# A graph network's edge loop on TensorE: the second layer's banks between the first layer's groups

## The chip, the core and the metric

One core of a Trainium2 chip runs the whole kernel in one launch. Its engines run side by side and wait for each other through semaphores: TensorE (PE in the profile; its weight loads have a row of their own, PEld) multiplies, VectorE (DVE) and ScalarE (ACT) work element by element, GpSimd (POOL) here issues the gathers, SyncE (SP) issues most other transfers. TensorE writes to PSUM, eight banks of 2 KB a partition; VectorE and ScalarE carry its results on to SBUF.

The metric is the device time of one execution in microseconds, as the median of several runs.

## The reference

A layer of message passing over a graph of 6250 nodes and 100000 edges, sorted by destination, with a residual and a normalisation behind it:

```python
row, col = edge_index[0], edge_index[1]                     # source, destination
msg_in = concatenate([x[row], x[col]], axis=-1)             # 100000 x 256
h = relu(msg_in @ Wm1 + bm1)                                # 256 wide
h = relu(h @ Wm2 + bm2)                                     # 256 wide
messages = h @ Wm3 + bm3                                    # 128 wide
agg = segment_sum(messages, col) / clip(count(col), 1)
upd = relu(concatenate([x, agg]) @ Wn1 + bn1) @ Wn2 + bn2
out = layernorm(x + (x + upd))
```

Everything is float32.

## The kernel before

The first layer's product is split: `x @ Wm1` is computed once for each node, for the source half (table `atab`, float32) and for the destination half (table `btab`, three bfloat16 terms that add up to a float32). This prologue takes about the first 90 us. Per edge the first layer is then a sum of two table rows. The third layer is linear, so it is applied after the sum over edges, once for each node.

The edges go in 196 groups of 512 (four tiles of 128), two groups a step, 98 steps; step p's stages are spread over several turns of the loop at L978, so that in one turn TensorE works on four steps. In turn p, TensorE does this, in the order in which it is written down (its order is the program's: `manual_schedule` holds PE from L285, ACT and POOL from L287 and DVE from L525 to it):

- **turning** (`turned`, L760, matmul L770) of step p-3: six transposes of the summed rows, 64 rows by 64 columns of the array each, into two banks; VectorE adds them to the accumulator `acc` (`pair_window`, L739, or `add_up`, L774);
- **node steps** of spot 0 (`node_steps`, L930): pieces of the work on finished nodes, dealt out from turn 34 on;
- **first layer** (`first_layer`, L660) of step p: for both groups the *rows*, 16 transposes a group of the gathered rows of `atab` into `ph` (L666), and then for both groups the *products* of `btab` rows with a one-hot matrix of the destinations, added in `ph` (L674, four a group in the early steps; L683, eight a group from step 59 on). `ph` takes four of the eight PSUM banks, two for each group, and there is one `ph`. ScalarE then applies bias and relu in two instructions, each over both groups (L692), into one of two tiles `h1`;
- **sums** (`summed`, L948; `pair_sums`, L729, matmul L734, in the last steps `sums`, L718, matmul L724) of step p-2: 16 matmuls, 32 columns of the array each, which add the edges of a window of nodes from `h2s`, four side by side. ScalarE copies the result (`part_of`, L748, copy L752);
- **second layer** (`second_layer`, L706, matmul L711) of step p-1: for each group two banks of eight matmuls on the whole array. VectorE takes each bank's maximum with the negated bias into `h2s` (L714), one tile for each group. Between the first group's two banks and the second's stand the node steps of spot 1.

The other four PSUM banks are handed out in turn by `bank()` (L562): whoever asks gets the bank that was handed out four calls before, and waits until that one's reader is done. A turn asks seven times (two for the turning, one for the sums, four for the second layer), more with node steps.

`fetch` (L598) issues the loads of step p+1 in turn p: eight gathers on POOL's queue (L607), four for each group, and four, later eight, loads of `btab` rows on SP's queue (L620). The first SP load waits for the last product that read the same buffer (two steps before). Three of the gathers also wait for a mark of TensorE (`MARKS`, L587), which keeps them in its pace: the first for the sums' last matmul, the fifth for a matmul at the start of the fourth bank, the seventh for the first product.

`follows` and `keep` (L572, L580) leave out waits that other waits already imply.

Of the kernel before, what the change touches and what calls it, by code (L numbers as in the profile page):

```python
# [20 lines left out]
P = 128  # L21
# [9 lines left out]
def kernel(  # L31
# [511 lines left out]
    with edge, tc.tile_pool(name="wk", bufs=2) as wk, tc.tile_pool(  # L543
# [116 lines left out]
        def first_layer(got, ohts, nts, step):  # L660
            for i, ((ag, _, _), nt) in enumerate(zip(got, nts)):
                for c in range(HC):
                    for j in range(GT):
                        for h in range(nt // 2):
                            half = slice(h * HP, (h + 1) * HP)
                            nc.tensor.matmul(ph[:, i, h, c, j * HP:(j + 1) * HP], ag[half, j, c * P:(c + 1) * P],  # L666
                                             ident[half, half], is_transpose=True, start=(c == 0 and j == 0),
                                             stop=False, skip_group_check=True)
            for i, ((_, bw, paired), nt) in enumerate(zip(got, nts)):
                for c in range(HC):  # L670
                    if paired:
                        for h in range(2):
                            half = slice(h * HP, (h + 1) * HP)
                            matmul = nc.tensor.matmul(ph[:, i, h, c, :], bw[half, 0, c * P:(c + 1) * P],  # L674
                                                      ohts[half, i, :], start=False, stop=True,
                                                      skip_group_check=True)
                            pace(step + 1, "products", (i * HC + c) * 2 + h, matmul)
                            last_product[step] = matmul
                        continue
                    for k in range(2):  # L680
                        for h in range(nt // 2):
                            half = slice(h * HP, (h + 1) * HP)
                            matmul = nc.tensor.matmul(ph[:, i, h, c, k * P:(k + 1) * P],  # L683
                                                      bw[half, k, c * P:(c + 1) * P],
                                                      ohts[half, i, k * P:(k + 1) * P], start=False, stop=True,
# [292 lines left out]
        for i in range(NP + 7):  # L978
# [42 lines left out]
            if p == 0:  # L1021
                whole(x_part(X_FIRST, bank, (nc.scalar, nc.vector)))
# [100 lines left out]
```

## Time and profile before

| | us |
|---|---|
| median of 3 runs | 1339.16 |
| lowest and highest | 1331.02, 1341.98 |
| the profiled execution, its own time | 1348.45 |
| its span, first to last instruction | 1346.7 |
| TensorE busy, of the span | 1237.1 |
| GpSimd busy | 793.6 |
| VectorE busy | 618.8 |
| ScalarE busy | 335.5 |
| mean granted TensorE clock | 0.976 |

Times inside the profile count from the span's start. In a row of the timeline stand the start, the length of what is merged in it, the engine, the line of the kernel, the operation, what it writes and reads, the shape, the number of instructions, and in brackets the engine's idle time before it with what ended it. A matmul's start is recorded and its end is modelled, and matmuls overlap, so the pitch from start to start tells more than the mean length. In the groups, "idle before" is the idle time of the engine just before such instructions. "Issue" means that the engine waited for nothing that the profile shows.

### The profile page before, as it was taken

The page shows a single profiled execution, that of the slowest core. Times are in us where ns is not written, and L with a number is a line of the kernel's source. Part 1 is how long each engine was busy: PE and PEld are TensorE (multiplying, and loading weights), DVE is VectorE, ACT ScalarE, POOL GpSimd, SP SyncE. Part 2 cuts the span into 40 slices and gives each one's busy share as a digit, 9 for nine tenths or more (in the row PEclk, how much of TensorE's full clock was granted, in tenths as well). Part 3 has the DMA queues.
Part 4 walks back from the last instruction along what each step waited for, and adds up shares of the span by engine and source line. Part 5 has one row for each costly group of instructions (what it writes and reads, how often), then busy time and mean ns, then how long its engine had stood idle before and what let it go on. Part 6 is the DMA issues. An engine that isn't in the chain of part 4 may idle for free.

```text
span 1346.7 us, 26320 instructions
## 1 busy us (share of the span) xinstructions
PE 1237.1 (92%) x10288; PEld 935.8 (69%) x10289; DVE 618.8 (46%) x1502; ACT 335.5 (25%) x500; POOL 793.6 (59%) x854
## 2 busy tenths in 40 slices
PE   8988998999999999999999998989988999999996
PEld 6746666776776667766766766767767677777784
DVE  6754333333333334443444443534445454555675
ACT  4741221122122112222221222221222212223232
POOL 6666665665666666666666665655655655556531
PEclk9999999999999999999999999999999899999998
DMA  7963443433433334334343444434444434344320
GB/s 224 336 207 105 124 116 99 114 106 101 112 108 112 101 107 115 106 108 129 108 110 113 123 114 118 134 111 125 131 115 120 123 111 137 107 118 122 108 58 24
DMA packets 113876, 163.66 MB, mean 122 GB/s; under 512 B 24730, under 2 KB 74592, under 8 KB 113728
## 3 DMA queue, kind: packets, MB, share of 16 engines
q0 software_dynamic: 38160, 103.75, 27.5%
q1 hardware_dynamic: 67292, 44.97, 10.8%
q10 hardware_dynamic: 8292, 13.18, 3.4%
q8 instruction: 82, 1.34, 0.4%
q14 instruction: 50, 0.41, 0.1%
HBM read 142.35 MB, written 19.86 MB: 120 GB/s over the span
## 4 chain that ended last, share of the span: by engine, by line
PE 89%; issue 6%; DVE 4%; DMA 0%; ACT 0%; POOL 0%; DVEq 0%; SPq 0%; ACTq 0%; POOLq 0%
PE bank L711 53%; PE bank L734 11%; PE ph L666 9%; PE bank L770 3%; PE ph L674 2%; PE pbt L315 2%; PE ph L683 2%; PE bank L844 2%; PE bank L811 1%; PE bank L817 1%; PE bank L724 1%; PE pxu L426 1%; DVE h L714 1%; DVE acc L779 0%; DVE span_i L267 0%
## 5 line engine op out<-in xcount | busy, mean ns | idle before, releaser
L607 POOL DMA_INDIRECT rows<-atab,srcT x784 | 746.1, 952 | 485.2 <-issue 166.8
L711 PE MATMUL bank<-w,h 128*128 128x256 f32 x3128 | 722.6, 386 | 8.0 <-DVE h L714 4.1
L711 PEld LDWEIGHTS bank<-w,h 128*128 128x128 f32 x3128 | 592.5, 192 | 139.3 <-issue 52.5
L714 DVE TENSOR_TENSOR h<-bank,nb 128x512 f32<-128x512 f32 x391 | 264.9, 690 | 600.8 <-PE bank L711 407.4
L692 ACT ACTIVATE h<-ph,b 128x1024 f32<-128x1024 f32 x194 | 205.6, 1110 | 789.2 <-remote 393.5
L666 PE MATMUL ph<-ident,rows 64*128 64x64 f32 x3128 | 134.6, 226 | 38.1 <-issue 36.6
L734 PE MATMUL bank<-h,oh 128*32 128x257 f32 x1312 | 155.5, 409 | 12.4 <-issue 1.3
L666 PEld LDWEIGHTS ph<-ident,rows 64*128 64x128 f32 x3128 | 117.2, 141 | 49.7 <-issue 46.5
L734 PEld LDWEIGHTS bank<-h,oh 128*32 128x32 f32 x1312 | 46.8, 112 | 93.8 <-issue 77.1
L743 DVE TENSOR_TENSOR acc<-acc,bank 128x96 f32 x328 | 83.5, 255 | 40.2 <-remote 18.4
L770 PEld LDWEIGHTS bank<-ident,part 64*128 64x128 f32 x681 | 31.1, 137 | 48.1 <-issue 27.6
L770 PE MATMUL bank<-ident,part 64*128 64x64 f32 x681 | 46.8, 237 | 12.6 <-DVE h L714 8.6
L315 PE MATMUL pbt<-w,xT 128*128 128x256 f32 x196 | 47.6, 388 | 5.9 <-DVE rest L340 3.0
L752 ACT COPY part<-bank 128x257 f32<-128x257 f32 x114 | 42.1, 375 | 24.4 <-PE bank L711 17.3
L315 PEld LDWEIGHTS pbt<-w,xT 128*128 128x128 f32 x196 | 36.5, 194 | 13.4 <-DVE rest L340 4.2
L674 PE MATMUL ph<-oht,rows 64*128 64x256 bf16 x472 | 40.1, 275 | 4.2 <-issue 4.2
L683 PE MATMUL ph<-oht,rows 64*128 64x128 bf16 x620 | 32.7, 225 | 10.7 <-issue 10.0
L642 DVE TENSOR_TENSOR oh<-iota_w,dloc 128x256 f32<-128x256 f32 x82 | 34.3, 418 | 0.0
L779 DVE TENSOR_TENSOR acc<-acc,bank 128x63 f32 x126 | 27.8, 221 | 13.3 <-remote 4.5
L683 PEld LDWEIGHTS <-rows 64*128 64x128 bf16 x620 | 23.2, 99 | 14.8 <-issue 14.7
L640 DVE TENSOR_SCALAR oht<-db,iota_p 128x512 bf16<-128x512 bf16 x98 | 31.8, 324 | 0.0
L674 PEld LDWEIGHTS <-rows 64*128 64x128 bf16 x472 | 24.4, 97 | 7.2 <-issue 6.3
(167 smaller groups left out, 613.0 us busy)
## 6 DMA issues: line engine op xcount, KB each, us to landing
rows<-btab SPq DMA_DIRECT2D x544, 32.0 KB
db<-reltab ACTq DMA_DIRECT2D x98, 128.0 KB
rows<-atab,srcT POOLq DMA_INDIRECT x784
btab<-acc SPq DMA_DIRECT2D x24, 384.0 KB
atab<-at SPq DMA_DIRECT2D x24, 256.0 KB
x_sb<-in_x_dram SPq DMA_DIRECT2D x5, 512.0 KB
xd<-in_x_dram SPq DMA_DIRECT2D x6, 256.0 KB
out_dram<-xd SPq DMA_DIRECT2D x6, 256.0 KB
```

Source lines behind the costliest of these rows:

```text
L315: nc.tensor.matmul(pbt[:, a, :], xT[:, (t0 + a) * P:(t0 + a + 1) * P], w1[:, k, :], start=True, stop=True)
L607: gather = nc.gpsimd.indirect_dma_start(out=ag[:, j, :], out_offset=None, in_=atab[:, :], in_offset=bass.IndirectOffsetOnAxis(ap=idx[:, j: ...
L666: nc.tensor.matmul(ph[:, i, h, c, j * HP:(j + 1) * HP], ag[half, j, c * P:(c + 1) * P], ident[half, half], is_transpose=True, start=(c == ...
L674: matmul = nc.tensor.matmul(ph[:, i, h, c, :], bw[half, 0, c * P:(c + 1) * P], ohts[half, i, :], start=False, stop=True, skip_group_check= ...
L683: matmul = nc.tensor.matmul(ph[:, i, h, c, k * P:(k + 1) * P], bw[half, k, c * P:(c + 1) * P], ohts[half, i, k * P:(k + 1) * P], start=Fal ...
L692: made = [nc.scalar.activation(h1[:, :, c, :].rearrange("p i (h e) -> p i h e", h=2), ph[:, :, :, c, :], AF.Relu, bias=b1[:, c:c + 1]) for ...
L711: matmul = nc.tensor.matmul(ph2[:, j - j0, :], h1[:, c, j * P:(j + 1) * P], w2[:, c, :], start=(c == 0), stop=(c == HC - 1))
L714: made = nc.vector.tensor_tensor(h2[:, j0:j0 + 2, :H], ph2, nb2.to_broadcast([P, 2, H]), op=ALU.max)
L734: matmul = nc.tensor.matmul(pg[(2 * i + q) * WN:(2 * i + q + 1) * WN, :H + 1], oh[:, 2 * q + k, :], h2[:, 2 * q + k, :], start=k == 0, sto ...
L743: made = nc.vector.tensor_add(window, window, pts[q // 2][:, 0, :, k:k + WN])
L752: copied.append(nc.scalar.copy(part[:nt * WN, i], pg[:nt * WN, :H + 1]))
L770: nc.tensor.matmul(pts[r][:, i, c, :], rows, ident[half, half], is_transpose=True, start=True, stop=True, skip_group_check=True)
```

## The change

The loop's turn is written in another order, and four functions are cut up for it; no instruction is added or taken away. `first_layer` becomes `first_group`, called once for each group (rows, then products of that group), and `relus`. `second_layer` becomes `second_bank` (eight matmuls) and `largest` (the VectorE part); the first group's two banks are now issued one by one. The order of TensorE in a turn is then:

turning, node steps of spot 0, first group's rows and products, **bank 1**, sums, **bank 2**, second group's rows and products, node steps of spot 1, **banks 3 and 4**.

With it move: `fetch` from behind the whole first layer to behind its first group; the relus to behind the second group, and so behind the sums' copy in ScalarE's order; the VectorE part of bank 1 to behind the sums; in turn 0 a piece of prologue work (`x_part`), and in the last turn the loading of window starts (`load_firsts`), from before the second group's banks to before the node steps of spot 1. The loop over further windows behind the main loop, which is skipped when no window needs it, calls the same functions.

```diff
         def first_layer(got, ohts, nts, step):
-            for i, ((ag, _, _), nt) in enumerate(zip(got, nts)):
...
+            for i in range(len(nts)):
+                first_group(i, got, ohts, nts, step)
+            return relus(nts, step)
+
+        def first_group(i, got, ohts, nts, step):
+            (ag, bw, paired), nt = got[i], nts[i]
+            for c in range(HC):
+                for j in range(GT):
+                    for h in range(nt // 2):
+                        half = slice(h * HP, (h + 1) * HP)
+                        nc.tensor.matmul(ph[:, i, h, c, j * HP:(j + 1) * HP], ag[half, j, c * P:(c + 1) * P],
+                                         ident[half, half], is_transpose=True, start=(c == 0 and j == 0),
+                                         stop=False, skip_group_check=True)
+            for c in range(HC):
+                if paired:
...
+        def relus(nts, step):
             h1 = next_h1()
...
         def second_layer(h1, h2, nt, step, before):
             for j0 in range(0, nt, 2):
...
+                largest(second_bank(h1, j0, step, before), h2, j0)
+
+        def second_bank(h1, j0, step, before):
+            ph2 = bank()
+            for j in range(j0, j0 + 2):
+                for c in range(HC):
+                    matmul = nc.tensor.matmul(ph2[:, j - j0, :], h1[:, c, j * P:(j + 1) * P],
+                                              w2[:, c, :], start=(c == 0), stop=(c == HC - 1))
+                    pace(step + 2, "second", before + j * HC + c, matmul)
+            return ph2
+
+        def largest(ph2, h2, j0):
+            made = nc.vector.tensor_tensor(h2[:, j0:j0 + 2, :H], ph2, nb2.to_broadcast([P, 2, H]), op=ALU.max)
+            follows("copied", made)
+            keep("largest", made)
...
-            if p < NP:
-                s = st[p]
-                s["h1"] = first_layer(s.pop("got"), s.pop("ohts"), s["nts"], p)
+            now = st[p] if p < NP else None
+            was = st[p - 1] if 0 <= p - 1 < NP else None
+            if now:
+                first_group(0, now["got"], now["ohts"], now["nts"], p)
             if i < NP:
                 st[i]["got"] = fetch(i, [(srcT[:, 2 * i + k, :], firsts[k]) for k in range(2)], [q for q, _ in queues],
                                      paces.pop(i, {}))
-            if p == 0:
-                whole(x_part(X_FIRST, bank, (nc.scalar, nc.vector)))
+            ph2 = second_bank(was["h1"][:, 0], 0, p, 0) if was else None
             if 0 <= p - 2 < NP:
                 pgs, matmul = summed(p - 2)
                 pace(p + 2, "sums", 0, matmul)
                 st[p - 2]["part"] = part_of(pgs, [GT] if p - 2 < PAIRED else st[p - 2]["nts"])
-            if 0 <= p - 1 < NP:
-                s = st[p - 1]
-                for j, nt in enumerate(s["nts"]):
-                    if p == NP and j == 1:
-                        load_firsts(NP - 2)
-                        load_firsts(NP - 1)
-                    second_layer(s["h1"][:, j], h2s[j], nt, p, j * GT * HC)
-                    if j == 0:
-                        node_steps(p, 1)
-            else:
-                node_steps(p, 1)
+            if was:
+                largest(ph2, h2s[0], 0)
+                largest(second_bank(was["h1"][:, 0], 2, p, 0), h2s[0], 2)
+            if now:
+                first_group(1, now.pop("got"), now.pop("ohts"), now["nts"], p)
+                now["h1"] = relus(now["nts"], p)
+            if p == 0:
+                whole(x_part(X_FIRST, bank, (nc.scalar, nc.vector)))
+            if p == NP:
+                load_firsts(NP - 2)
+                load_firsts(NP - 1)
+            node_steps(p, 1)
+            if was:
+                second_layer(was["h1"][:, 1], h2s[1], was["nts"][1], p, GT * HC)
             if p in (1, 2):
                 clear(2)
```

53 lines of the change are left out of this document (17 added, 36 removed).

## The prediction

> **What bounds the kernel now.** I read the page first (shares of the engines, the chain that ended last), then the groups of TensorE in the main loop (100 to 1300 us), then single steps in the timeline.
>
> ```profile
> span 1346.7 us, 26320 instructions
> PE 1237.1 (92%) x10288; PEld 935.8 (69%) x10289; DVE 618.8 (46%) x1502; ACT 335.5 (25%) x500; POOL 793.6 (59%) x854
> PE 89%; issue 6%; DVE 4%; DMA 0%; ACT 0%; POOL 0%; DVEq 0%; SPq 0%; ACTq 0%; POOLq 0%
> ```
>
> TensorE (PE) carries the chain: 89% its own work, 6% "issue", time in which it waited for nothing that the profile shows. No transfer and no other engine sets the end. But is PE at its peak while it is busy? The groups of the loop (columns: count, busy us, mean ns of one, idle us before them and what ended it):
>
> ```profile
> L711 PE MATMUL bank<-w,h 128*128 128x256 f32 x3055 | 703.6, 386 | 4.3 <-DVE h L714 4.1
> L734 PE MATMUL bank<-h,oh 128*32 128x257 f32 x1312 | 155.5, 409 | 12.4 <-issue 1.3 <-DVE acc L743 0.9
> L666 PE MATMUL ph<-ident,rows 64*128 64x64 f32 x3040 | 130.7, 226 | 36.3 <-issue 36.0
> L770 PE MATMUL bank<-ident,part 64*128 64x64 f32 x636 | 44.5, 238 | 12.6 <-DVE h L714 8.6 <-DVE xd L847 2.0 <-DVE rce L813 1.4
> L674 PE MATMUL ph<-oht,rows 64*128 64x256 bf16 x456 | 38.9, 275 | 4.2 <-issue 4.2
> L683 PE MATMUL ph<-oht,rows 64*128 64x128 bf16 x608 | 31.9, 225 | 10.7 <-issue 10.0
> ```
>
> Now one step early in the loop (start, length, times; in brackets the pause before), and below it one that began after a long wait:
>
> ```profile
> 415.22 0.40 PE L770 MATMUL bank<-ident,part 64*128 64x64 f32 x6
> 415.45 0.48 PE L666 MATMUL ph<-ident,rows 64*128 64x64 f32 x10
> 416.12 0.30 PE L666 MATMUL ph<-ident,rows 64*128 64x64 f32 x3 [0.19 <-issue]
> 416.84 0.78 PE L666 MATMUL ph<-ident,rows 64*128 64x64 f32 x19 [0.42 <-issue]
> 417.46 0.60 PE L674 MATMUL ph<-oht,rows 64*128 64x256 bf16 x8
> 417.99 2.70 PE L734 MATMUL bank<-h,oh 128*32 128x257 f32 x16
> 420.62 7.17 PE L711 MATMUL bank<-w,h 128*128 128x256 f32 x32
> 427.73 0.28 PE L770 MATMUL bank<-ident,part 64*128 64x64 f32 x2
> ```
>
> ```profile
> 711.01 0.27 PE L770 MATMUL bank<-ident,part 64*128 64x64 f32 x1
> 712.28 0.39 PE L770 MATMUL bank<-ident,part 64*128 64x64 f32 x5 [1.00 <-DVE xd L847]
> 712.45 1.22 PE L666 MATMUL ph<-ident,rows 64*128 64x64 f32 x32
> 713.45 0.66 PE L674 MATMUL ph<-oht,rows 64*128 64x256 bf16 x8
> 714.03 1.08 PE L734 MATMUL bank<-h,oh 128*32 128x257 f32 x16
> 715.04 1.13 PE L711 MATMUL bank<-w,h 128*128 128x256 f32 x4
> ```
>
> The same work: six turning transposes, 32 row transposes, 8 products, 16 sums, then the 32 matmuls of the second layer's four banks. Up to the second layer the first step needs 5.40 us (415.22 to 420.62). In the other, a wait of over a microsecond stood in front, and everything behind it to the second layer took 2.76 us (712.28 to 715.04): no pauses, and the sums 1.08 us instead of 2.70. So the short matmuls aren't slow in themselves; they run out. I read this as the supply of instructions: 61 matmuls and their weight loads come in 2.8 us, after 32 matmuls of 0.22 us in which the supply gets ahead, but by a bounded amount: here six and ten matmuls ran before the first pause. The wait at 711 gave it more time. What the bound is, the trace does not say.
>
> The price of all pauses, from the groups: the sums' 82 blocks of 16 cost (155.5 + 12.4) / 82 = 2.05 us against 1.08, that is 79 us; the row transposes' idle 36 us, the products' 4.2 + 10.7 = 15 us, the turning's 12.6 us. Together 143 us of the loop. This is the most that an order of the same instructions can win in these places.
>
> **The change part by part.** Each step runs the same instructions. Instead of one run of 62 short matmuls, then four banks, TensorE now has: turning (6) and the first group's rows (16 transposes, 4 products, later 8), bank 1, sums (16), bank 2, the second group's rows (20, later 24), banks 3 and 4.
>
> *What is recovered.* The sums follow a bank of 8 slow matmuls and are 16, as long as the run before the pause above (6 + 10): I take four fifths of 79, 63 us, not all, since one bank stands ahead of them instead of four. The first run is 26 and the second 20, both beyond 16: I take half of the 51 us of rows and products, 26 us. The turning's waits on the copies out of the banks (8.6 us by L714) go, since a bank's copy now has the second group's rows as well to hide behind: 8 us. Sum 97 us; bounds 0 and 143.
>
> *What the added switches cost.* Three times more often in a step TensorE goes from one shape of tile to another. Nearest rows:
>
> ```profile
> 414.91 0.38 PE L711 MATMUL bank<-w,h 128*128 128x256 f32 x1
> 415.22 0.28 PE L770 MATMUL bank<-ident,part 64*128 64x64 f32 x2
> 417.79 0.27 PE L674 MATMUL ph<-oht,rows 64*128 64x256 bf16 x2
> 417.99 0.42 PE L734 MATMUL bank<-h,oh 128*32 128x257 f32 x3
> 420.62 0.48 PE L711 MATMUL bank<-w,h 128*128 128x256 f32 x1
> ```
>
> From the second layer to 64-row work: 0.31 us from start to start, where the layer's own pitch is (7.17 - 0.38) / 31 = 0.22, so 0.09. From the products to the sums: 0.20 against (0.60 - 0.27) / 7 = 0.05, so 0.15. The second layer's first matmul after other work is 0.48 long against 0.38, 0.10 more. Rows to bank, twice, are in no row; I price them as products to sums plus that 0.10: 0.25 each. Bank to sums and bank to rows: 0.09 each, like bank to turning. Products to sums falls away: -0.15. Sums to bank stays. In all 0.25 + 0.25 + 0.09 + 0.09 - 0.15 = 0.53 us a step, over 97 steps 51 us. Bounds: 0, where a switch falls into a pause that is there anyway; three of the dearest (0.31 + 0.10 each), 1.23 us a step, 119 us.
>
> *What is late next.* The relus (L692) read both groups' rows, so they now start behind the second group, and the next step's first rows overwrite what they read. The bank of the third copy (L714) is wanted again by the next step's first bank, four banks on.
>
> ```profile
> 420.25 2.12 ACT L692 ACTIVATE h<-ph,b 128x1024 f32<-128x1024 f32 x2 [10.12 <-remote]
> 1045.29 0.23 PE L683 MATMUL ph<-oht,rows 64*128 64x128 bf16 x2 [0.51 <-issue]
> 1045.61 2.12 ACT L692 ACTIVATE h<-ph,b 128x1024 f32<-128x1024 f32 x2 [7.92 <-PE ph L683]
> 416.88 1.29 DVE L714 TENSOR_TENSOR h<-bank,nb 128x512 f32<-128x512 f32 x2 [2.16 <-PE bank L770]
> 412.90 0.95 POOL L607 DMA_INDIRECT rows<-atab,srcT  x1 [0.30 <-issue]
> 414.16 0.95 POOL L607 DMA_INDIRECT rows<-atab,srcT  x1 [0.31 <-issue]
> ```
>
> The relus need 2.12 us. Their cover is two banks (16 x 0.22 = 3.5), a switch (0.25) and the turning (0.31 + 0.23): 4.3 us. They begin 0.32 us behind the last product late in the loop (1045.29 to 1045.61), which is hidden with 1.9 us to spare, but 2.46 us early in it (417.79 to 420.25), which is 0.3 us too late. I count 0, since I expect signals to come sooner once the pauses shrink. Without that cover the full 2.4 us would stand in each step.
>
> *The rest at nothing.* The first copy out of a bank (DVE, L714) now waits for the sums too, because it overwrites what they read; behind it are only the next copies, and bank 2 (1.7 us) covers it. The sums' copy on ScalarE goes ahead of the relus instead of behind: 0.4 us, done during bank 2. The node steps' work keeps its place ahead of banks 3 and 4; its ScalarE part queues behind the relus and is wanted steps later. The gathers are written down earlier, but wait for the same marks of TensorE: eight starts of 1.26 us (412.90 to 414.16) are 10.1 us a step, the next bound on POOL's queue, and a step stays above that. SP's loads wait for the last product of the step before and are wanted a step later.
>
> Sum: 1348.45 of the profiled execution - 97 + 51 = 1302; its span is 1346.7, the rest lies around it. The median of the runs is 1339.16, 9.3 lower, so 1293.
>
> **The rivals.**
> 1. All pauses go: 1339 - 143 + 51 = 1247. For it: the step at 712, where 61 short matmuls ran through. Against: only after an extra wait; else the first pause came after 16. [...]
> 2. The supply is bounded by number, not by order. A step of 94 matmuls and 94 loads takes 427.73 - 415.22 = 12.51 us, 67 ns an instruction. If that is a fixed price, pauses only move, the switches fall into them, and the time stays 1339. Against: 122 instructions came in 2.76 us at 712. [...]
> 3. Late signals. If L714 stays as late as at 416.88, its bank is free 2.3 us after the turning starts (416.88 + 0.65 - 415.22), while the next bank 1 would start after 0.23 + 0.50 + 0.19 + 0.25 = 1.2 us: a wait of 1.1 us in the 57 early steps (456 products in blocks of 8), 63 us: 1356.
> 4. Slower: the switches cost their 51 us and nothing is recovered, as one bank is too little for the supply to get ahead: 1390. It decides where less than 51 of the 143 us, 36%, comes back. For it: after four banks only 16 matmuls ran unbroken, so after one perhaps four. [...]
>
> **How the numbers follow.** Forecast 0.42, rival 1 0.15, rival 2 0.12, rival 3 0.10, rival 4 0.21. About 1% is what a measurement of this kernel can tell from no change: 1326 to 1353. Faster: 0.42 + 0.15 = 0.57. Same: rival 2 and part of 3, 0.16. Slower: rival 4 and the rest of 3, 0.27. Predicted is the likeliest, 1293; its own range is 1255 (more recovered) to 1325 (switches at twice the price). With the others, 1240 to 1385 leaves out the lower part of rival 1 and somewhat more than half of rival 4, under 2 in 10.
>
> **What would show it.** Right: sums of about 1.1 to 1.4 us in one piece behind the first bank; L734's busy time near 100 instead of 155.5; "issue" before L666 halved; starts of about 0.3 us at bank to sums and bank to rows. Wrong: pauses inside the sums or between a bank's matmuls; L666 waiting for ACT L692 (rival 3), or L711 for DVE L714; the step still at 12.3 us with pauses elsewhere (rival 2). The forecast fails above all if a single bank does not let the supply get ahead.

## The result, and the profile after

| | before | after |
|---|---|---|
| median, same chip, 4 runs each | 1337.35 us | 1377.74 us |
| the profiled execution, its own time | 1348.45 | 1377.59 |
| TensorE busy | 1237.1 | 1250.5 |
| mean granted TensorE clock | 0.976 | 0.949 |

The ratio is 1.032, with an interval of 1.025 to 1.039: slower, where the prediction said 1293 us. The page of the changed kernel: span, the engines' busy time, and the shares of the chain of work that ended last.

```profile
span 1375.8 us, 26421 instructions
PE 1250.5 (91%) x10288; PEld 918.9 (67%) x10289; DVE 613.3 (45%) x1502; ACT 339.7 (25%) x500; POOL 793.8 (58%) x854
PE 86%; issue 7%; DVE 4%; ACT 1%; DMA 1%; another core or an unknown queue 1%; POOL 0%; DVEq 0%; ACTq 0%; SPq 0%; POOLq 0%
```

TensorE still carries the chain, and "issue" has not shrunk. TensorE's groups between 100 and 1340 us (count, busy us, mean ns | idle us before and what ended it), where L720 is the second layer, L671 the rows, L746 the sums, L678 and L687 the products, L782 the turning, L698 the relus and L726 the copies out of the banks:

```profile
L720 PE MATMUL bank<-w,h 128*128 128x256 f32 x3072 | 777.4, 402 | 14.5 <-issue 13.7 <-DVE h L726 0.3 <-DVE acc L755 0.2
L671 PE MATMUL ph<-ident,rows 64*128 64x64 f32 x3064 | 140.0, 233 | 63.4 <-issue 58.2 <-ACT h L698 5.2
L746 PE MATMUL bank<-h,oh 128*32 128x257 f32 x1312 | 96.3, 410 | 0.3 <-issue 0.3
L678 PE MATMUL ph<-oht,rows 64*128 64x256 bf16 x458 | 47.0, 281 | 3.1 <-issue 3.0
L687 PE MATMUL ph<-oht,rows 64*128 64x128 bf16 x620 | 32.0, 220 | 0.5 <-issue 0.5
```

The sums do what was forecast: 96.3 us instead of 155.5, with 0.3 us of idle time instead of 12.4. The products' pauses are gone too (3.6 us instead of 14.9). But the rows stand idle for 63.4 us instead of 36.3, and the second layer's matmuls, the same in number, are busy for longer: 402 ns each instead of 386. One step shows why: TensorE, then ScalarE, then VectorE, then GpSimd.

```profile
413.83 0.72 PE L671 MATMUL ph<-ident,rows 64*128 64x64 f32 x16
414.38 0.38 PE L678 MATMUL ph<-oht,rows 64*128 64x256 bf16 x4
414.70 3.72 PE L720 MATMUL bank<-w,h 128*128 128x256 f32 x16
418.35 0.40 PE L782 MATMUL bank<-ident,part 64*128 64x64 f32 x6
421.51 0.71 PE L671 MATMUL ph<-ident,rows 64*128 64x64 f32 x16 [2.77 <-issue]
...
422.37 1.99 PE L720 MATMUL bank<-w,h 128*128 128x256 f32 x8
...
419.34 2.12 ACT L698 ACTIVATE h<-ph,b 128x1024 f32<-128x1024 f32 x2 [6.13 <-PE bank L782]
...
419.43 1.29 DVE L726 TENSOR_TENSOR h<-bank,nb 128x512 f32<-128x512 f32 x2 [4.80 <-PE bank L782]
...
417.00 0.95 POOL L607 DMA_INDIRECT rows<-atab,srcT  x1 [0.30 <-issue]
419.71 0.94 POOL L607 DMA_INDIRECT rows<-atab,srcT  x1 [1.76 <-PE bank L782]
```

The second group's products end at 414.76, but the relus that read them start at 419.34, 4.58 us later, when banks 3 and 4 and the turning have run as well. In the same tenth of a microsecond VectorE gets bank 3, the first eight of the sixteen matmuls from 414.70, together with bank 4, and at 419.71 GpSimd gets the mark that its next gather waits for: the signals come in one burst. The relus end at 421.46, and at 421.51 the next rows, which overwrite `ph`, start. "Issue" hides this: the profile links only 5.2 us of the rows' wait to L698, but 36 of the loop's steps have rows that start within 0.2 us of the relus' end.

I added up TensorE's times from start to start over the loop of both traces, sorted by the kinds of the two matmuls:

```
us of the loop, start to start           before   after
sums to sums                              146.0    76.3
rows to rows                              148.8   101.0
products to products                       61.1    32.7
turning to rows                             4.7    71.4
second layer to second layer              672.4   684.6   (2976 and 2835 pitches)
switches between two kinds, all that
  changed, net                                 -     +86.9
turning, node steps                        79.9    88.9
```

The first three rows, where the pauses stood, give back 69.7 + 47.8 + 28.4 = 145.9 us. The switches cost 86.9 us, of which 141 x 0.216 = 30.5 would have been paid as plain pitches: 56.4. The new wait costs 66.7. The second layer's own pitches cost 12.2 + 30.5 = 42.7 more: 130 of them instead of 34 take 0.427 us, half clock (the granted clock reads 0.50 in the bank from 460.00, in the last section), which is 96 x 0.211 = 20 us, and 22.7 us are other longer pitches. The rest of the table adds 9.0. In sum 1348.45 - 145.9 + 56.4 + 66.7 + 42.7 + 9.0 = 1377.4, against 1377.59 profiled.

These entries are not quite what their names say. On the chips where nothing pauses (below), the same sums over the traces of the two orders (the old one without marks) show 14.5 us less in the first three rows too, because some of their pitches become switches, and 14.6 us more in the second layer beyond plain pitches. So about 131 of the 145.9 us are pauses that went, and of the 22.7 us only some 8 are new pauses between a bank's matmuls; the price of the switches stays at 56.

### The profile page after: what moved, and what is told of

The parts are those of the page before. It is cut to its first block, busy times and chain, and to the rows that moved or that the text cites. A ratio compares the mean times of both kernels' runs of the same rounds, so it can differ in the third digit from the quotient of the medians.

```text
span 1375.8 us, 26421 instructions
## 1 busy us (share of the span) xinstructions
PE 1250.5 (91%) x10288; PEld 918.9 (67%) x10289; DVE 613.3 (45%) x1502; ACT 339.7 (25%) x500; POOL 793.8 (58%) x854
## 4 chain that ended last, share of the span: by engine, by line
PE 86%; issue 7%; DVE 4%; ACT 1%; DMA 1%; another core or an unknown queue 1%; POOL 0%; DVEq 0%; ACTq 0%; SPq 0%; POOLq 0%
PE bank L720 54%; PE ph L671 9%; PE bank L746 6%; PE bank L782 3%; PE ph L678 2%; PE pbt L315 2%; PE bank L856 2%; PE bank L829 2%; PE bank L823 2%; PE ph L687 1%; PE bank L736 1%; PE pxu L426 1%; DVE acc L791 0%; ACT h L698 0%
## 5 line engine op out<-in xcount | busy, mean ns | idle before, releaser
L720 PE MATMUL bank<-w,h 128*128 128x256 f32 x3128 | 790.5, 401 | 14.8 <-issue 13.7
L720 PEld LDWEIGHTS bank<-w,h 128*128 128x128 f32 x3128 | 595.6, 197 | 176.8 <-issue 89.0
L726 DVE TENSOR_TENSOR h<-bank,nb 128x512 f32<-128x512 f32 x391 | 262.1, 688 | 507.0 <-PE bank L720 192.1
L698 ACT ACTIVATE h<-ph,b 128x1024 f32<-128x1024 f32 x194 | 205.5, 1110 | 416.5 <-PE bank L720 121.3
L671 PE MATMUL ph<-ident,rows 64*128 64x64 f32 x3128 | 143.7, 232 | 67.5 <-issue 61.1
L671 PEld LDWEIGHTS ph<-ident,rows 64*128 64x128 f32 x3128 | 118.7, 144 | 108.0 <-issue 98.6
L746 PE MATMUL bank<-h,oh 128*32 128x257 f32 x1312 | 96.3, 410 | 0.3 <-issue 0.3
L746 PEld LDWEIGHTS bank<-h,oh 128*32 128x32 f32 x1312 | 37.2, 117 | 52.1 <-issue 30.0
L782 PEld LDWEIGHTS bank<-ident,part 64*128 64x128 f32 x681 | 31.8, 137 | 50.7 <-issue 32.6
L782 PE MATMUL bank<-ident,part 64*128 64x64 f32 x681 | 48.6, 237 | 14.2 <-DVE rce L825 4.5
L678 PE MATMUL ph<-oht,rows 64*128 64x256 bf16 x472 | 48.5, 281 | 3.3 <-issue 3.0
L687 PE MATMUL ph<-oht,rows 64*128 64x128 bf16 x620 | 32.0, 220 | 0.5 <-issue 0.5
L824 DVE SCALAR_TENSOR_TENSOR bank<-acc,b,bank 128x256 f32<-128x256 f32 (+1 forms) x25 | 12.0, 478 | 39.8 <-PE bank L720 32.4
L859 DVE TENSOR_TENSOR xd<-xd,bank 128x256 f32<-128x256 f32 x12 | 5.1, 421 | 52.5 <-PE bank L720 43.6
```

The source lines that it names most:

```text
L698: made = [nc.scalar.activation(h1[:, :, c, :].rearrange("p i (h e) -> p i h e", h=2), ph[:, :, :, c, :], AF.Relu, bias=b1[:, c:c + 1]) for ...
L720: matmul = nc.tensor.matmul(ph2[:, j - j0, :], h1[:, c, j * P:(j + 1) * P], w2[:, c, :], start=(c == 0), stop=(c == HC - 1))
L726: made = nc.vector.tensor_tensor(h2[:, j0:j0 + 2, :H], ph2, nb2.to_broadcast([P, 2, H]), op=ALU.max)
L746: matmul = nc.tensor.matmul(pg[(2 * i + q) * WN:(2 * i + q + 1) * WN, :H + 1], oh[:, 2 * q + k, :], h2[:, 2 * q + k, :], start=k == 0, sto ...
L782: nc.tensor.matmul(pts[r][:, i, c, :], rows, ident[half, half], is_transpose=True, start=True, stop=True, skip_group_check=True)
```

## The experiments

Each was timed against the kernel before on the same chip. That matters: on five chips the kernel before took 1336 to 1351 us, on two others 1149 to 1150. Ratios are to the kernel before.

**The relus by group (two runs).** In the first, each group's relus are two instructions of their own, the first group's right behind its products; in the second they are cut as well but all stand behind the second group.

```diff
                 first_group(0, now["got"], now["ohts"], now["nts"], p)
+                now["h1"] = next_h1()
+                group_relus(now["h1"], 0, now["nts"][0], p)
...
-                now["h1"] = relus(now["nts"], p)
+                group_relus(now["h1"], 1, now["nts"][1], p)
```

> The changed kernel with the relus cut by group: two of 128x512 for the first group right behind its products, two for the second group behind its own, instead of two of 128x1024 for both groups at the end. The next step's first rows then wait for relus that run several microseconds earlier. Theory A (the loss is the wait of the first rows for the late relus, 71 us from turning to rows, and the half clock that follows it): turning to rows falls from 71 to about 6 us, the half-clock excess in the second layer from 27 to under 15, the time to 1290 to 1310. Theory B (the loss is the price of the added switches of shape, and the wait only stands where the supply of instructions would pause anyway): the time stays above 1350 and the idle time turns up elsewhere. Theory C (the late signal itself is the limit): the wait moves to the next thing that needs a signal, the copies out of the banks or the rows of the second group, and the time is 1330 to 1350.

> The changed kernel with the relus cut by group but all four still behind the second group. The first rows of the next step wait for the first two (about 1.3 us of ScalarE) instead of both of 1.11 us, with the same signal. Theory A: about 0.9 us less wait in the 36 steps in which rows started right behind the relus' end, 30 us: 1340 to 1350. Theory B: no change, 1370 to 1385. If the late signal is the larger part of the wait, this run gains little and the run with the relus moved gains most.

Measured: 1354.07 us, ratio 1.014 (1.011 to 1.018), and 1400.18, ratio 1.046 (1.042 to 1.051). Where the relus' work behind the last product is halved, the time falls by 24 us against the changed kernel's 1377.74 (another chip, the kernel before within 0.2%); where it is only cut, it grows by 22. From turning to rows the loop spends 57.5 and 97.6 us. Neither run came out as a theory had it: the first is above theory A's 1310 with most of the wait still there, the second above all that was expected, and why a mere cut costs 22 us is open. In the first run the rows still wait, and now the profile names it:

```profile
L671 PE MATMUL ph<-ident,rows 64*128 64x64 f32 x3080 | 138.6, 229 | 48.5 <-ACT h L697 45.7 <-issue 1.4
```

The two groups share one tile `ph`, and in the program the first group's rows wait for the relus of both.

**Another place for the second group, and both groups in front (two runs).** In the first, the second group's rows stand ahead of bank 2; in the second, both groups stand in front and only bank 1 is left ahead of the sums.

```diff
                 largest(ph2, h2s[0], 0)
-                largest(second_bank(was["h1"][:, 0], 2, p, 0), h2s[0], 2)
             if now:
                 first_group(1, now.pop("got"), now.pop("ohts"), now["nts"], p)
                 now["h1"] = relus(now["nts"], p)
+            if was:
+                largest(second_bank(was["h1"][:, 0], 2, p, 0), h2s[0], 2)
```

```diff
-                first_group(0, now["got"], now["ohts"], now["nts"], p)
+                now["h1"] = first_layer(now.pop("got"), now.pop("ohts"), now["nts"], p)
...
-            if now:
-                first_group(1, now.pop("got"), now.pop("ohts"), now["nts"], p)
-                now["h1"] = relus(now["nts"], p)
```

> The changed kernel with the second group's rows and products right behind the sums, ahead of bank 2 instead of behind it. The relus get one bank, 1.73 us, more cover (6.0 instead of 4.3 us), and one change of shape less a step. Theory A: relus that end 4.8 + 2.1 us behind the last product are still about 1 us late, so the wait falls from 67 to 20 to 35 us and the switches by 0.2 us x 97 = 20 us: 1310 to 1335. Theory B: only the switches, 1355 to 1365.

> One part of the change alone: both groups' rows and products in one run as before the change, then bank 1, sums, banks 2 to 4. The relus keep a cover of four banks and the sums. Two changes of shape more than before the change, (0.20 + 0.10 + 0.31 - 0.22 - 0.15) = 0.24 us a step, 23 us. Theory A (no relu wait here; a bank ahead of the sums gives the supply its time): the sums' blocks take about 0.8 us instead of 1.8, 70 us less; the time is 1285 to 1310. Theory B (supply cannot be won by order): 1340 to 1365, the pauses in the rows grow by what the sums lose.

Measured: 1357.44, ratio 1.015 (1.011 to 1.018), and 1403.59, ratio 1.050 (1.046 to 1.053). The turning's group of the first, then the rows' and products' of the second:

```profile
L782 PE MATMUL bank<-ident,part 64*128 64x64 f32 x681 | 56.0, 242 | 68.4 <-DVE h L726 35.3 <-issue 22.3 <-DVE rce L825 2.8
```

```profile
L671 PE MATMUL ph<-ident,rows 64*128 64x64 f32 x3008 | 155.4, 225 | 75.6 <-issue 75.3
L678 PE MATMUL ph<-oht,rows 64*128 64x256 bf16 x456 | 48.0, 278 | 24.9 <-issue 24.9
```

With a bank more of cover most of the wait for the relus goes (from turning to rows 14.1 us; in 18 steps rows still start within 0.2 us of the relus' end), and the turning waits instead for the copies out of the banks, which are late in the same way. With both groups in one run the sums are quick (80.2 us from start to start), and the pauses stand in the rows and products, larger than before the change (75.6 and 24.9 us against 36.3 and 4.2), though three banks stand ahead of that run. So a bank in front is not enough; the run has to be short as well. By time the first run lies in theory B's range, but its wait did move, as theory A had it; the second lies above both of its theories, with pauses in the rows as theory B had them.

**The wait taken away in earnest, a control, and a wait added (three runs).** `ph` and `h1` become two tiles each, one for each group; the control does the same in the old order; the third adds a wait of bank 4's first matmul for the first relu.

```diff
-        ph = p1.tile([P, 2, 2, HC, 2 * P], F32, name="ph")
+        ph = [p1.tile([P, 2, HC, 2 * P], F32, name=f"ph{i}") for i in range(2)]
...
-        next_h1 = in_turn(wk, 2, [P, 2, HC, GE], F32, "h1")
+        h1_of = [in_turn(wk, 2, [P, HC, GE], F32, f"h1{i}_") for i in range(2)]
```

```diff
+                    if straight[0] and relu and before and j == 2 and c == 0:
+                        tc.add_manual_dep(
+                            matmul.ins, relu.pop().ins.name,
+                            mybir.DependencyInfo(mybir.DependencyClass.Sync, mybir.DependencyReason.DATA),
+                            reason="the fourth bank waits for the first relu")
```

> The changed kernel's order, with the relus cut by group (the first group's right behind its products) and with ph and h1 as two tiles each, one for each group, so that the next step's first rows need only the first group's relus. Theory A (the changed kernel lost its gain to the wait of the next rows for relus that start late): the time from the turning to the rows, 71.4 us of the loop, falls to about 5, the pitches at half clock that follow the waits go from 130 to under 50, and the time is 1377.7 - 66 - 15 = about 1295. Rival B (the late signals of TensorE are what costs, and every reader of a bank or of ph has them): the wait goes to the copies out of the banks, as in the run with the second group's rows a bank earlier; TensorE waits 50 us or more for L726's copies, and the time is 1340 to 1360.

> The kernel before, its order unchanged, with the relus cut by group and two tiles each for ph and h1: the control for the run above. Theory A: nothing in the old order waits for the relus (the turning to the rows takes 4.7 us in all), so the time stays, within 1% of before, 1325 to 1350. Rival B: the same, or some us less through an earlier start of the first group's relus. If it is faster by over 2%, the two tiles are worth something without the new order, and the run above has to be read against this one.

> The changed kernel with one wait more: the first matmul of bank 4 waits for the first relu instruction. It asks what brings TensorE's signals out. Theory A1 (signals are held back while TensorE's sequencer runs ahead, and come as soon as it meets a wait that is not yet fulfilled): the relus start 0.3 to 1.0 us behind the last product in all steps, bank 4 starts at most 0.5 us late (97 x 0.4 = 39 us), the wait of the rows (67 us) shrinks below 15, and the time is 1340 to 1365. Theory A2 (signals come only when the matmuls queued behind have run): the relus start 1.5 to 2.6 us behind the last product, bank 4 stands for 1 to 2 us in each step, and the time is 1420 to 1480.

Measured: 1347.76, ratio 1.009 (1.006 to 1.013); the control 1337.19, ratio 1.001 (0.998 to 1.003); the added wait 1441.22, ratio 1.079 (1.075 to 1.083). The rows and the turning in the first run, and the second layer in the third:

```profile
L671 PE MATMUL ph<-ident,rows 64*128 64x64 f32 x3064 | 146.7, 228 | 29.5 <-issue 24.9 <-DMA rows<-atab,srcT 4.3
L780 PE MATMUL bank<-ident,part 64*128 64x64 f32 x681 | 52.9, 238 | 31.1 <-DVE rce L823 7.9 <-issue 6.8 <-DVE xd L857 6.2
```

```profile
L722 PE MATMUL bank<-w,h 128*128 128x256 f32 x3071 | 799.9, 406 | 149.1 <-ACT h L699 133.3 <-issue 13.4 <-DVE acc L762 0.9
```

With two tiles the step from turning to rows costs 9.7 us instead of 71.4 and the second layer 668.6 instead of 684.6. So the wait was real and was caused by the relus: 30 us come back. Theory A's 1295 does not: rows to rows costs 130.8 instead of 101.0 and the turning 57.4 instead of 38.8. Rival B is the nearer, though the waits went mostly to other places than the copies. The third run has theory A2's time and its wait of bank 4 (133.3 / 97 = 1.4 us a step), but not its delays: the relus start 1.0 to 2.0 us behind the last product in 47 of 90 steps and 3.0 us or more in 41, and in these TensorE had mostly stood idle for 2 us or more when the relus started. So a wait that TensorE meets does not by itself bring the signals out, and they can be late while no matmul runs.

**Without the marks, and a chip of another sort (six runs on two chips).** The marks that keep gathers in TensorE's pace fall away in the loop; each gather then waits only for the rows that it overwrites. First in the order with two tiles, in the old order and in the changed kernel; then the first of these again, the changed kernel as it is, and the kernel before with each transpose of the turning issued twice.

```diff
-            if (stage, n) in MARKS:
+            if (stage, n) in MARKS and i == 1:
```

```diff
-                        nc.tensor.matmul(pts[r][:, i, c, :], rows, ident[half, half], is_transpose=True,
+                        for _ in range(2 if straight[0] else 1):
+                            nc.tensor.matmul(pts[r][:, i, c, :], rows, ident[half, half], is_transpose=True,
```

> The run with two tiles each for ph and h1, and without the marks of TensorE in the loop: a gather then waits only until the rows that it overwrites are read (its first four for the first group's rows two turns back, the next four for the second group's), not for the sums, the fourth bank and the first product. Theory A (with the relus' wait gone the rows wait for gathers, which wait for marks that come late: L671's 29.5 us of idle time and the chain's 21% on L607): L671's idle time falls under 10, GpSimd leaves the chain, and the time is 1347.8 - 20 to 40, that is 1305 to 1328. Rival C (the rows' pauses are TensorE's own, a supply bounded by number): the idle time before L671 stays at 25 us or more and the time is 1335 to 1360.

> The kernel before, without the marks in the loop: the control for the run above. Theory A and rival C: in the old order GpSimd is off the chain (0%), so the time stays within 1%, 1325 to 1350. If the marks held gathers apart from other transfers, it is slower; if it is faster by over 2%, the run above has to be read against this one.

> The changed kernel, without the marks in the loop. Theory A: the wait for the late relus stands ahead of the gathers here, so nothing is won: the turning to the rows stays at 60 to 75 us and the time at 1365 to 1390. If instead gathers were what held the rows, that stretch falls by half and the time is under 1345.

> The kernel before with each transpose of the turning issued twice (same result): 6 matmuls and 6 weight loads a step more, 97 steps. Theory N (where this program takes about 1337 us, TensorE's instructions come at a fixed price each, about 63 ns a matmul or load, so that a step of 188 costs 12 us in any order): 12 x 63 ns x 97 = 73 us more, 1410, on a chip where the kernel before takes 1337; and on a chip where it takes 1149, where TensorE is never short of instructions, only the array's time, 6 x 0.035 x 97 = 20 us more, 1170. Theory O (the pauses depend on the order, a short run running out behind slow matmuls): on a chip of 1337 the six stand right behind 32 slow matmuls, with a supply in hand, and cost about the array's 20 us or a little more, 1345 to 1370.

> The changed kernel, unchanged, beside the kernel before, on whatever chip these runs get. The two chips so far gave the kernel before 1336 and 1149 us. On one of 1149: theory S (there the switches stand alone) 1149 + 97 x 0.5 = about 1198, with no wait of the rows and the relus 0.3 us behind the last product. On one of 1336: about 1378 again, with 60 to 75 us between the turning and the rows.

> The changed order with two tiles each for ph and h1 and without the marks once more, on whatever chip these runs get. Theory N on a chip of 1336: with the relus' wait and the gathers' marks both gone the loop still doesn't fall below 1225 us, because the instructions are the same in number; the time is 1330 to 1360 and pauses stand inside the rows, the sums or the banks. Theory A on such a chip: 1290 to 1325. On a chip of 1149: 1199 again.

Both sets of three went to chips where the unchanged kernel before takes 1148.65 and 1149.70 us. There the runs took 1198.71, 1149.65, 1197.61, and then 1165.98 (twice the turning), 1197.61 (the changed kernel as it is: ratio 1.042, 1.040 to 1.043) and 1198.35. The changed kernel as it is, on such a chip: page, groups, one step of TensorE and the relus in it.

```profile
span 1196.1 us, 26421 instructions
PE 92%; DVE 4%; DMA 1%; issue 1%; ACT 1%; POOL 0%; DVEq 0%; SPq 0%; ACTq 0%; POOLq 0%
```

```profile
L720 PE MATMUL bank<-w,h 128*128 128x256 f32 x3096 | 740.4, 387 | 0.6 <-DVE acc L755 0.3 <-DVE xT L830 0.3
L671 PE MATMUL ph<-ident,rows 64*128 64x64 f32 x3055 | 132.0, 226 | 0.0
L746 PE MATMUL bank<-h,oh 128*32 128x257 f32 x1312 | 88.3, 386 | 0.0
```

```profile
400.14 0.71 PE L671 MATMUL ph<-ident,rows 64*128 64x64 f32 x16
400.69 0.39 PE L678 MATMUL ph<-oht,rows 64*128 64x256 bf16 x4
...
410.55 0.71 PE L671 MATMUL ph<-ident,rows 64*128 64x64 f32 x16
...
401.12 1.11 ACT L698 ACTIVATE h<-ph,b 128x1024 f32<-128x1024 f32 x1 [2.36 <-PE ph L678]
```

And the old order there, in the run without marks (1149.65, the same as with them): one step.

```profile
401.86 0.40 PE L770 MATMUL bank<-ident,part 64*128 64x64 f32 x6
402.09 1.16 PE L666 MATMUL ph<-ident,rows 64*128 64x64 f32 x32
403.08 0.60 PE L674 MATMUL ph<-oht,rows 64*128 64x256 bf16 x8
403.62 1.08 PE L734 MATMUL bank<-h,oh 128*32 128x257 f32 x16
404.62 7.17 PE L711 MATMUL bank<-w,h 128*128 128x256 f32 x32
411.73 0.40 PE L770 MATMUL bank<-ident,part 64*128 64x64 f32 x6
```

On these chips nothing pauses in the old order: 62 short matmuls run through in 404.62 - 401.86 = 2.76 us, as the step behind the long wait did in the trace of before. The relus start 0.04 us behind the products (400.69 + 0.39 to 401.12) instead of 4.58. What is left of the change is its switches: a step grows from 411.73 - 401.86 = 9.87 us to 410.55 - 400.14 = 10.41, that is by 0.54 us, and the kernel by 1197.61 - 1149.70 = 47.9. The two tiles change nothing there (1198.71 and 1198.35), because nothing is late. The theories for the runs without marks were written for the other sort of chip; two of these runs were made there as well (below), the changed kernel without marks was not.

**The open ones, on chips of the first sort (two runs, then one and one).** Twice the turning and the two tiles without marks once more; then the old order without marks; then the old order with two marks moved to matmuls that give a signal anyway.

```diff
-        MARKS = {("sums", 0): 0, ("second", 12): 4, ("products", 0): 6}
+        MARKS = {("sums", 0): 0, ("second", 11): 4, ("products", 7): 6}
```

> The kernel before with the turning twice, again, for a chip where the kernel before takes 1336 us. Theory N (a fixed price of about 63 ns for each matmul and load): 73 us more than the kernel before, about 1410. Theory O (pauses by order): 16 us more, as on the chip of 1149, or a little over, 1345 to 1370. On a chip of 1149: 1166 again.

> The changed order with two tiles each and without the marks, again, for a chip where the kernel before takes 1336 us. Theory N: not below the kernel before, 1330 to 1360, with the loop at 1225 us or more. Theory A (nothing but the relus and the gathers held it): 1290 to 1325. On a chip of 1149: 1198 again.

> The kernel before without the marks, again, for a chip where the kernel before takes 1336 to 1346 us. Without the marks each gather waits for its own row transposes, so TensorE gives 1626 to 1700 signals instead of 1005, in the same order of work. Theory Q (on such a chip each signal of TensorE costs its sequencer some 60 ns, as the 38 us between the two runs with two tiles suggest): 620 x 60 ns = 37 us more, 1375 to 1385, or more pauses in the rows, where the new signals are given. Theory D (there the run without marks lost to its gathers, which stand close together in the way of other transfers, or to an order in which signals count for nothing): within 1% of the kernel before. On a chip of 1149: 1149 again, and the question stays open.

> The kernel before with two of the three marks moved to matmuls that give a signal anyway: the fifth gather waits for the end of bank 3 instead of the start of bank 4, the seventh for the last product of the early steps instead of the first. TensorE's instructions with a signal fall from 1258 to 1101. The run without marks had more of them and took a third longer. Theory Q2 (on a chip of 1336 us the lateness of TensorE's signals grows with their number, and the time with it): the relus start sooner than 1.46 us on the mean behind the last product, and the time is 1300 to 1330. Theory D2 (the number counts for nothing; the run without marks lost through the place of its signals, or through gathers): within 1%, 1325 to 1350. On a chip of 1149: 1149, and the question stays open.

Measured, with the kernel before of the same chip: 1361.43 against 1346.36 (1.010, 1.007 to 1.013); 1391.10 against 1346.36 (1.034, 1.030 to 1.037); 1784.36 against 1336.52 (1.333, 1.327 to 1.338); 1364.14 against 1351.12 (1.010, 1.006 to 1.014).

Twelve more instructions a step cost 15 us, as on the other sort of chip (16 us): theory N, a fixed price of 63 ns each, falls, and with it the prediction's second rival in its form of a fixed price for every instruction. The two tiles without marks are slower than with them (1.009) and above what either theory gave, so theory A falls as well. The old order without marks shows the late signals at their worst; its group of the second layer, then one wait in TensorE's and ScalarE's timeline:

```profile
L711 PE MATMUL bank<-w,h 128*128 128x256 f32 x3063 | 873.1, 440 | 272.9 <-ACT part L752 187.5 <-issue 77.5 <-DVE h L714 4.4
```

```profile
408.88 1.08 PE L734 MATMUL bank<-h,oh 128*32 128x257 f32 x16
409.89 5.59 PE L711 MATMUL bank<-w,h 128*128 128x256 f32 x24
418.31 3.63 PE L711 MATMUL bank<-w,h 128*128 128x256 f32 x8 [2.83 <-issue]
...
417.88 0.38 ACT L752 COPY part<-bank 128x257 f32<-128x257 f32 x1 [5.77 <-remote]
```

The sums end at 409.96; their copy on ScalarE starts at 417.88, 7.92 us later, and bank 4, which takes the sums' bank, waits for that copy. TensorE stands still for a signal of its own. The same program took 1149.65 us on a chip of the other sort. Both theories for this run missed by far. With fewer signals (counted in the traces, 951 of TensorE's instructions give one instead of 1108) the relus come forward, from 1.46 us behind the last product on the mean to 0.86, but not the time: the rows' idle time is 50.1 us where it was 36.3, theory Q2's 1300 to 1330 is not reached, and theory D2's 1% is just missed. So the number of signals alone does not decide the time.

Nor does this run show that their number moves the relus, because its edit moves gathers too: the seventh now starts behind the last early product instead of the first. The traces tie late relus to gathers. In the trace of before, 40 of 96 relus start 2 to 3 us behind the last product's start, and all 40 start 0.86 to 0.93 us behind the end of a gather. In the changed kernel the 29 latest start 1.16 to 1.48 us behind one, with three or four gathers running or issued between product and relus. With the marks moved, 77 of 96 steps have no gather in between, and their relus start 0.19 us behind the product on the mean, those of the other 19 steps 2.0. And in the run without marks the eight gathers of the step above are issued in one row, 407.90 to 417.62, and the copy starts 0.26 us behind it. On the other sort of chip gathers lie in between in 64 of 95 steps of the changed kernel, and the relus start 0.04 us behind the product all the same. Whether gathers hold the signals back there, or gathers and relus both wait for signals that something else holds, no run separates: none moves gathers and leaves the signals. That stays the open rival.

## Why the prediction was wrong

*What is recovered* was mis-sized on the low side: 97 us forecast, with bounds of 0 and 143; 145.9 came off the three rows of the table, about 131 of it pauses. One bank was enough here to let 16 to 24 short matmuls run through (idle time of 0.3 us before the sums, 3.6 before the products). That is the prediction's first rival in this step.

*What the added switches cost* held: 51 us forecast, 0.53 a step; the profiled loop shows 56.4, and the chip without pauses 0.54 a step and 47.9 us in all.

*What is late next* is the step that failed: "I count 0, since I expect signals to come sooner once the pauses shrink." They come later. From the last product's start to the relus' start it is 1.46 us on the mean before and 2.8 after, with two clusters, 1.0 to 2.0 us (49 of 95 steps) and 4.5 to 6.0 (29). The step's own arithmetic had the two sides, a cover of 4.3 us against 2.46 + 2.12, already 0.3 us short; it put the wait at nothing on an expectation, and had no place for a delay longer than the one it saw. Measured, the wait costs 66.7 us and the additional half clock about 20. Why the signals are later in the new order stays open; the late relus go with the gathers, which the prediction left at nothing because they wait for the same marks. The two tiles show that it is this wait, and that the old order does not have it (control 1.001). The prediction had named the sign, "L666 waiting for ACT L692", but gave the late signals 1.1 us a step and a chance of 0.10.

*The rest at nothing* held while the rows waited for the relus. With that wait taken away it holds no longer: rows and turning took 30 and 19 us more. In the chain between 400 and 460 us of the run with two tiles GpSimd's gathers are a fifth:

```profile
by line: PE bank L718 37.1%; POOL rows L607 21.0%; issue 18.5%; PE ph L671 6.8%; PE bank L744 5.0%; PE bank L780 4.8%; DMA rows<-atab,srcT 4.3%; PE ph L678 2.2%; another core or an unknown queue 0.2%; POOLq L607 0.1%
```

That the gathers' late marks are the whole of it was only argued; taking the marks away made that order slower.

Of the rivals, the fourth came nearest in time (1390) by a way that did not happen, since the pauses did go. That the measured 1377.74 lies in the wide range, 1240 to 1385, is therefore luck: the range reached that far mainly for this rival. The third, late signals, had the right mechanism in the wrong place: on L714's banks, where it appears once the relus have more cover (35.3 us on L726 with the rows a bank earlier). The second falls with the doubled turning: 26 ns for each matmul more with its load, against its 67 ns for each instruction. What no part of the prediction held is that the pauses, the whole gain to be had, may not exist on another chip: there the change can only cost its switches, 4.2%.

## What to carry to other kernels

Before work is moved between a producer and the engine that frees its buffer, take the longest delay from the producer's end to the consumer's start that the trace shows, and assume it at every new place; a cover that is smaller than that delay plus the consumer's work is a wait. Here this would have shown the sign, 0.3 us a step, and not the size, because the delay itself grew. Cut a shared buffer into one tile for each group before the groups are pulled apart, or both wait for both, as the rows did here (45.7 us on the relus with one `ph`; with two, 9.7 us from turning to rows instead of 71.4). And repeat the baseline on another chip before an order is chosen against pauses that the profile calls "issue": here the switches cost 56.4 us on the one sort of chip and 47.9 on the other, and pauses to win back, some 131 us, stood only on the first.

## What the runs showed of the hardware

- **Two sorts of chip.** The same program, the kernel before, takes 1336 to 1351 us on five chips and 1149 to 1150 on two. On the two, TensorE does not pause between short matmuls (0.0 us of idle time before the rows and the sums of the changed kernel) and its consumers start at once (mean 0.3 us from the last product's start, changed kernel without marks). Which property of the chip or of its set-up does that, no run here shows, and each chip was measured at one time only.
- **Signals that wait.** On chips of the first sort, a consumer of TensorE can start some microseconds behind the end of the matmul that it waits for (4.58 and 7.92 us in the two waits shown), and in the first of these two consumers start within 0.1 us of each other (419.34 and 419.43). With banks 3 and 4 behind the last product it is 4.5 to 6.0 us in 29 of 95 steps, and as much in 31 steps of the run in which bank 4 is held back. The late ones go with gathers (0.86 to 0.93 us behind the end of one in 40 steps of before); the cause is not shown.
- **The price of a matmul more.** Twice the turning costs (1361.43 - 1346.36) / (97 x 6) = 26 ns for each matmul more with its weight load, 28 on the other sort of chip. Both hold for matmuls added behind 32 slow ones.
- **Half clock after some waits.** One of the longer waits in the changed kernel, and what follows:

```profile
455.07 0.40 PE L782 MATMUL bank<-ident,part 64*128 64x64 f32 x6
458.53 1.12 PE L671 MATMUL ph<-ident,rows 64*128 64x64 f32 x16 [3.06 <-issue]
459.44 0.64 PE L678 MATMUL ph<-oht,rows 64*128 64x256 bf16 x4
460.00 3.78 PE L720 MATMUL bank<-w,h 128*128 128x256 f32 x8
```

A bank takes 3.78 us behind an idle 3.06 us, where it takes 1.99 else; behind the 2.77 us at 421.51 the bank at 422.37 took 1.99. The granted clock reads 0.50 over the first of these banks (460.00 to 463.78) and 1.00 over the other (422.37 to 424.36). The trace does not give one length of idle time for this: half clock stands behind 3.06 us as the profile counts it, but also behind waits of 1.55 to 2.03 us (the four that end at 392.9, 634.6, 901.1 and 968.0; 0.50 to 0.54 in the banks behind them), and not behind 2.92 and 2.97 us (the two that end at 306.1 and 511.0; 1.00 in the banks behind them).
